# Graph network, first layer: both halves of the features from one window of rows, the own half through DRAM, in a new order of issue

## The chip, the cores and the metric

The kernel runs on one core of one Trainium2 chip. The metric is the device time of one execution in microseconds (us). The time before is the median of seven runs; the profile is one more execution, recorded by the hardware profiler. Engines are named as the profile does: PE (matmul), PEld (its weight load), DVE, ACT, POOL and SP.

## The reference, cut to what matters

There are 12500 nodes with 256 features each and 200000 edges, sorted by destination `dst`. The first layer works in four heads of 32 columns:

```
feat      = relu(x @ W[o] + b[o])          # o = 0: own half (128 columns), o = 1: neighbour half
att_s     = leaky(sum_k feat_self * a_self)          # one number a node and head
att_n     = leaky(sum_k feat_nei  * a_neigh)
edge_w    = (att_s[src] + att_n[dst]) * edge_weight
agg[src] += edge_w * feat_nei[dst]                   # segment sum over edges
y         = concat(headnorm(feat_self), headnorm(agg))
x1        = layernorm(x + y)
```

The second layer computes `relu(x1[src] @ W_a + x1[dst] @ W_b + b)` for each edge, sums it by `dst`, puts the sum and x1 through an update matrix, a relu and two layer norms. So the own half is needed once a node, the neighbour half once an edge, at `dst`.

## The kernel before, in words

Everything runs in three stages one after the other.

**Stage 1, by groups of edges.** The edges are cut into 112 groups (`NG`) of 14 tiles of 128. As edges are sorted by `dst`, all destinations of a group lie in a window of 128 consecutive rows of `x`, which starts at a row number read into a register (`base_reg`, L211). For each group `sort_tasks` (L548) sorts the edges by block of `src`: one-hot tables `A`, `B`, `Z` (`hot` L568, `hot_b` L572, `pair` L576, `reach` L615), counts on PE (`ranks`, `begins`), 14 place look-ups on ACT (`place_pick` L651), the split of a place into quotient and rest (`split` L658 to L660), the one-hot tables of these (`hot_r` L664, `hot_q` L674, `goods` L669), and the target rows `ix` (`index` L644). Then `message` (L718) multiplies a one-hot table `oT` (`hot_n` L709) with the window's neighbour features, `evict` (L725) copies the result out of PSUM, and `scatter` (L731) writes it with four indirect DMAs a group, issued by POOL, to rows `ix` of a log in DRAM. The buffer `ix` has four copies: `index` of group g waits for the scatters of group g-4.

Beside this, `feat_tasks` (L440) computes features. In every step it takes two sets of 128 rows: the window `xw` of group g, for the neighbour half, and block g of 128 nodes `xb`, for the own half. Each is loaded (L432, L438), transposed by PE (L457, L460), copied from PSUM (`keep` L466) and multiplied with its half of the weights (`project` L471, L474). From `relu` (L482) on the two halves lie side by side in one tile of 256 columns: `att_mult` (L486), `mean_sum` (L491), `att_sum` (L495), `centre` (L500). The own half of `F` goes to `selfd` in DRAM by blocks (`out_f` L528), the own attention to the resident tile `atts` (`leaky_s` L525), and the neighbour half is split into three bf16 parts (`part` L514 to L520). There are 112 groups, but only 98 blocks (`NB`): in the last 14 steps there is no `xb`, and the tiles are 128 columns wide.

The order of issue on PE, ACT, DVE and SP is written out by hand: the dictionary `AT` (L40) gives every step of a group a due time, group g stands `TG` = 256 units after group g-1, and all steps are issued in the order of due time:

```
t0 = TG * g
work[t0 + AT[name]].append(f)
for t in sorted(work): ...
```

So one period of 256 units holds one step of each name, of different groups. Every eighth group also brings the steps `m_...`, which prepare the edge lists of the next eight groups. Each engine takes its instructions in that order and waits where an operand is not there yet.

**Stage 2, by blocks of nodes.** For each block of 128 nodes the log is read back (`log_load` L951), expanded (`log_hot` L959, L964) and summed by PE (`log_sum` L972). Four blocks make a batch: `load_y` (L1076) reads `x` and the own half from `selfd`; `own_s` to `own_d` (L1091 to L1124) normalize the own half; `heads_a` (L983) multiplies the sum with `atts` and adds the rest; then follow norms, the projection for the second layer, and the stores of `x1d` and `pd`.

**Stage 3, the second layer,** gathers rows of `pd` by `src` (L1346), and works by groups of edges again (L1370 to L1424).

The functions that the diff touches, and what calls them:

Of the kernel before, what the change touches and what calls it, by code (L numbers as in the profile page):

```python
# [11 lines left out]
def _warn_once_fixed(msg, *args, **kwargs):  # L12
# [28 lines left out]
    "widen": -453, "hot": -365, "hot_b": -265, "pair": -179, "ranks": -86, "quarter": -64, "rows": -29,  # L41
    "begins": 13, "keep_begins": 55, "keep_v": 51, "shift": 161, "reach": 262, "steps": 227, "steps_keep": 243,
    "steps_low": 256, "target": 313, "index": 400, "place_mm0": 52, "place_mm1": 63, "place_mm2": 204,
    "pick0": 73, "pick1": 78, "pick2": 78, "pick3": 87, "pick4": 123, "pick5": 144, "pick6": 156, "pick7": 170,
    "pick8": 179, "pick9": 219, "pick10": 229, "pick11": 239, "pick12": 249, "pick13": 280, "split": 339,
    "hot_r": 358, "goods": 374, "hot_q": 371, "permute": 424, "rel_keep": 435, "extras": 477, "rel_turn": 502,
    "rel_row": 552, "rel_out": 574, "rel_in": 595, "hot_n": 959, "message0": 997, "evict0": 1053,
    "message1": 1032, "evict1": 1063, "message2": 1056, "evict2": 1082, "message3": 1065, "evict3": 1121,
    "message4": 1101, "evict4": 1165, "message5": 1188, "evict5": 1203, "scatter0": 1120, "scatter1": 1146,
    "scatter2": 1197, "scatter3": 1206, "load": -331, "transposes": 47, "keep": 68, "project": 80, "relu": 295,  # L50
    "att_mult": 355, "mean_sum": 459, "att_sum": 438, "centre": 467, "leaky_n": 498, "part0": 584, "part1": 636,
    "part2": 665, "part3": 705, "leaky_s": 585, "out_f": 634, "m_load": -1689, "m_cast0": -1234,
    "m_cast1": -1433, "m_col0": -1201, "m_keep0": -1125, "m_col1": -698, "m_keep1": -614, "m_col2": -941,
    "m_keep2": -861, "m_block": -1073, "m_place": -877, "m_high": -378, "m_rest": -285, "m_mid": 263,
    "m_low": 351, "m_win": -76, "m_turn": -866, "m_pairs": -710, "m_mask": -535, "m_count": 210,
# [45 lines left out]
def kernel(  # L101
# [45 lines left out]
    selfd = dram.tile([ROWS, HD], FT, name="selfd")  # L147
# [12 lines left out]
    atts = consts.tile([P, NB, H], FT, name="atts")  # L160
# [49 lines left out]
    def base_reg(g):  # L210
        return nc.sync.value_load(basei[0:1, g:g + 1], min_val=0, max_val=N - P)  # L211
# [4 lines left out]
    with ExitStack() as l0:  # L216
# [208 lines left out]
        xb = {}  # L425
        F3 = {}

        def load_group(g):
            if g < NG:
                b = base_reg(g) if g else 0  # L430
                xw[g] = xin.tile([P, D], FT, name="xw")
                nc.sync.dma_start(xw[g], x[bass.ds(b, P), :])  # L432
            if g < NB:
                xb[g] = xin.tile([P, D], FT, name="xb")
                n = min(P, N - g * P)
                if n < P:
                    nc.vector.memset(xb[g], 0.0)
                nc.sync.dma_start(xb[g][:n], x[g * P:g * P + n, :])  # L438

        def feat_tasks(g):  # L440

            ww, bb = g < NG, g < NB
            o0, o1 = (0 if bb else 1), (2 if ww else 1)
            lo, hi = o0 * HD, o1 * HD
            st = {}

            def flat(t):
                return t[:, lo:hi]

            def heads(t):  # L450
                return t[:, lo:hi].rearrange("p (a k) -> p a k", k=32)

            def transposes():
                tp = ps.tile([P, 512], FT, name="tp", bufs=1)
                if ww:
                    for c in range(2):
                        nc.tensor.transpose(tp[:, c * P:(c + 1) * P], xw[g][:, c * P:(c + 1) * P], ident)  # L457
                if bb:
                    for c in range(2):
                        nc.tensor.transpose(tp[:, (2 + c) * P:(3 + c) * P], xb[g][:, c * P:(c + 1) * P], ident)  # L460
                st["tp"] = tp

            def keep():
                xT = feat.tile([P, 4, P], FT, name="xT")
                a, z = (0 if ww else 2), (4 if bb else 2)
                nc.scalar.copy(xT[:, a:z].rearrange("p c q -> p (c q)"), st["tp"][:, a * P:z * P])  # L466
                st["xT"] = xT

            def project():
                fp = bank[g][:, 0:D] if ww else ps.tile([P, 512], FT, name="fs")[:, 0:D]  # L470
                nc.tensor.matmul(fp[:, lo:hi], ones3, bias3[:, lo:hi], start=True, stop=False)  # L471
                for o in range(o0, o1):
                    for c in range(2):
                        nc.tensor.matmul(  # L474
                            fp[:, o * HD:(o + 1) * HD], st["xT"][:, (2 + c) if o == 0 else c, :],
                            w0s[:, c, o * 4:(o + 1) * 4, :].rearrange("p a k -> p (a k)"),
                            start=False, stop=(o == o1 - 1 and c == 1))
                st["fp"] = fp

            def relu():  # L480
                st["R"] = feat.tile([P, D], FT, name="R")
                nc.scalar.activation(flat(st["R"]), st["fp"][:, lo:hi], AF.Relu)  # L482

            def att_mult():
                st["tm"] = feat.tile([P, D], FT, name="tm")
                nc.vector.tensor_tensor(flat(st["tm"]), flat(st["R"]),  # L486
                                        atb.rearrange("p o h k -> p (o h k)")[:, lo:hi], op=OP.mult)

            def mean_sum():
                st["m"] = feat.tile([P, 2 * H], FT, name="m")  # L490
                nc.vector.tensor_reduce(st["m"][:, o0 * H:o1 * H], heads(st["R"]), AX.X, OP.add)  # L491

            def att_sum():
                st["a"] = feat.tile([P, 2 * H], FT, name="a")
                nc.vector.tensor_reduce(st["a"][:, o0 * H:o1 * H], heads(st["tm"]), AX.X, OP.add)  # L495

            def centre():
                st["F"] = feat.tile([P, D + H], FT, name="F", bufs=4)
                m = st["m"][:, o0 * H:o1 * H]
                nc.vector.scalar_tensor_tensor(  # L500
                    heads(st["F"]), m[:, :, None].to_broadcast([P, (o1 - o0) * H, 32]), -1.0 / 32, heads(st["R"]),
                    op0=OP.mult, op1=OP.add)

            def leaky_n():
                a = st["a"][:, H:2 * H]
                nc.vector.scalar_tensor_tensor(st["F"][:, D:D + H], a, 0.2, a, op0=OP.mult, op1=OP.max)


            def part(k):
                def f():  # L510
                    n = st["F"][:, HD:]
# [11 lines left out]
            def leaky_s():  # L523
                a = st["a"][:, 0:H]
                nc.vector.scalar_tensor_tensor(atts[:, g, :], a, 0.2, a, op0=OP.mult, op1=OP.max)  # L525

            def out_f():
                nc.sync.dma_start(selfd[g * P:(g + 1) * P, :], st["F"][:, 0:HD])  # L528

            w = lambda f: f if ww else None  # L530
            k = lambda f: f if bb else None
            return dict(transposes=transposes, keep=keep, project=project, relu=relu,
                        att_mult=att_mult, mean_sum=mean_sum, att_sum=att_sum, centre=centre, leaky_n=w(leaky_n),
                        part0=w(part(0)), part1=w(part(1)), part2=w(part(2)), part3=w(part(3)),
                        leaky_s=k(leaky_s), out_f=k(out_f))
# [262 lines left out]
        work = defaultdict(list)  # L798
        for name, fs in (("hot_b", (first_nodes, lambda: load_group(1), load_norm_consts, bias_parts, bases)),
# [4 lines left out]
            work[min(AT[name], AT["split"] - 1) + 0.5] += fs  # L804
# [5 lines left out]
        for g in range(max(NG, NB)):  # L810
            t0 = TG * g
            if g < NG:
                for name, f in sort_tasks(g).items():
                    put_in(t0, name, f)
# [4 lines left out]
            if g % GC == 0 and 0 < g < NG:  # L819
# [98 lines left out]
    with ExitStack() as bar:  # L918
# [64 lines left out]
        def heads_a(q):  # L983
# [4 lines left out]
                                    atts[:, b:b + n, :, None].to_broadcast([P, n, H, 32]), op=OP.mult)  # L988
# [87 lines left out]
        def load_y(q):  # L1076
            b, n = spans[q]
            y = ys[q] = bw.tile([P, BB, D], FT, name="y", bufs=4)
            fs[q] = bw.tile([P, BB, HD], FT, name="fs")
            m = min(n, N // P - b)  # L1080
            if m < n:
                nc.vector.memset(y[:, m], 0.0)
                nc.sync.dma_start(y[:N % P, m], x[(b + m) * P:N, :])
            if m:
                nc.sync.dma_start(y[:, :m], x[b * P:(b + m) * P, :].rearrange("(b p) w -> p b w", p=P))
            nc.sync.dma_start(fs[q][:, :n], selfd[b * P:(b + n) * P, :].rearrange("(b p) w -> p b w", p=P))
# [4 lines left out]
        def own_s(q):  # L1091
            b, n = spans[q]
            own[q] = bw.tile([P, BB, HD], FT, name="oq", bufs=1), bw.tile([P, BB * H], FT, name="ov")
            nc.scalar.activation(own[q][0][:, :n], fs[q][:, :n], AF.Square)
# [12 lines left out]
        def own_c(q):  # L1107
            b, n = spans[q]
            v = own.pop(q)[1]
            F3 = fs[q][:, :n].rearrange("p b (h k) -> p (b h) k", h=H)  # L1110
            nc.vector.reciprocal(v[:, :n * H], v[:, :n * H])
            nc.vector.tensor_tensor(F3, F3, v[:, :n * H, None].to_broadcast([P, n * H, 32]), op=OP.mult)
# [6 lines left out]
        def own_d(q):  # L1119
            b, n = spans[q]  # L1120
            F = fs.pop(q)[:, :n]
# [569 lines left out]
```

## Time and profile before

| what | value |
|---|---|
| median of 7 runs | 4378.88 us (4370.61 to 4387.98) |
| the profiled execution's own time | 4374.71 us |
| its span, first to last instruction | 4372.8 us, so 1.9 us lie around it |
| stage 1, to the first matmul of stage 2 | 0 to 1081 us |
| stage 2, to its last matmul L972 | 1081 to 1992 us |
| stage 3, first L1424 to last instruction | 2019 to 4373 us |
| whole span, busy | PE 84%, DVE 72%, ACT 54%, POOL 61% |
| stage 1 from 50 to 1040 us, busy | PE 96%, DVE 97%, ACT 99%, POOL 53%, granted clock 1.00 |
| stage 2, busy | PE 100%, DVE 95%, ACT 24%, POOL 67%, granted clock 1.00 |
| stage 3, busy | PE 75%, DVE 54%, ACT 47%, POOL 63%, granted clock 0.87 |

In such a table a busy share is the union of the times in which some instruction of the engine runs. Two instructions of one engine overlap by some tens of nanoseconds in the records, so what an instruction costs its engine is the time from its start to the start of the next one; this is read from the timeline, where each line has start, duration, engine, source line, operation, output and inputs.

### The profile page before, as it was taken

The numbers are of one execution on the slowest core, as the hardware profiler recorded it, in microseconds if no ns is written. First come the engines' busy times: TensorE is split into PE (matmuls) and PEld (weight loads), VectorE is DVE, ScalarE is ACT, GpSimd is POOL, SyncE is SP. The second block draws the span as 40 slices with busy tenths as digits, with TensorE's granted clock in tenths as the row PEclk, the third lists the DMA queues.
The fourth block names the chain that finished last, engine by engine and source line by source line (L and its number), as shares of the span: only waits on it lengthen the run. The fifth ranks groups of instructions, "written<-read, shape, count | busy, mean of one in ns | idle before, by whom it ended". The sixth has DMA issues, their size and how long they took to land. (4 is left out here: it accounts for less than half of the span.)

```text
span 4372.8 us, 82564 instructions
## 1 busy us (share of the span) xinstructions
PE 3684.7 (84%) x24976; PEld 3120.0 (71%) x24976; DVE 3165.7 (72%) x9205; ACT 2374.0 (54%) x8379; POOL 2657.8 (61%) x2542
## 2 busy tenths in 40 slices
PE   8999999997999999996777777777777777777776
PEld 6888888876888888885666666666666666666665
DVE  9999999997999999995555555555555555555555
ACT  8999999996122222223444444444444444444444
POOL 2555455555666666664666666666666666666664
PEclk9999999998999999998888888889889888888888
DMA  6777766666666666664555555555555555555554
GB/s 200 273 271 265 250 220 214 216 203 222 180 192 192 191 191 191 189 187 134 143 143 148 145 144 143 147 144 142 146 144 147 145 143 146 144 146 143 144 145 113
DMA packets 470160, 763.55 MB, mean 175 GB/s; under 512 B 76203, under 2 KB 313505, under 8 KB 469713
## 3 DMA queue, kind: packets, MB, share of 16 engines
q1 hardware_dynamic: 339552, 415.13, 33.0%
q0 software_dynamic: 110848, 327.87, 24.4%
q10 hardware_dynamic: 19312, 15.21, 1.1%
q8 instruction: 204, 3.34, 0.3%
q14 instruction: 244, 1.99, 0.1%
HBM read 559.81 MB, written 198.12 MB: 173 GB/s over the span
## 5 line engine op out<-in xcount | busy, mean ns | idle before, releaser
L1346 POOL DMA_INDIRECT gb<-pd,srcf x1563 | 1500.7, 960 | 857.0 <-issue 505.9
L1424 PE MATMUL agg<-gb,o 128*128 128x256 f32 x3126 | 938.8, 428 | 286.0 <-ACT gb L1407 200.6
L1405 DVE TENSOR_TENSOR gb<-qp,gb 128x512 f32<-128x512 f32 x781 | 531.6, 681 | 651.1 <-remote 146.9
L1424 PEld LDWEIGHTS agg<-gb,o 128*128 128x128 f32 x3126 | 645.5, 215 | 458.3 <-ACT gb L1407 253.0
L731 POOL DMA_INDIRECT log<-m,ix x448 | 542.0, 1210 | 528.7 <-ACT m L725 149.9
L972 PE MATMUL sum<-lg,o 128*128 128x256 f32 x3724 | 838.9, 379 | 12.4 <-DVE o L964 12.2
L1407 ACT ACTIVATE gb<-gb 128x512 f32<-128x512 f32 x781 | 487.2, 627 | 631.2 <-DVE gb L1405 412.3
L972 PEld LDWEIGHTS sum<-lg,o 128*128 128x128 f32 x3724 | 696.4, 189 | 112.1 <-POOL lg L959 11.9
L964 DVE TENSOR_SCALAR o<-iotap,lg 128x128 f32<-128x128 f32 x1862 | 612.8, 398 | 42.8 <-PE sum L972 33.6
L651 ACT ACTIVATE junk<-wp,nbig 128x99 bf16<-128x99 f32 x1568 | 602.6, 458 | 0.8 <-PE wp L624 0.7
L1383 PE MATMUL qp<-qh,oT 128*128 128x256 f32 x1563 | 592.9, 398 | 6.2 <-PE agg L1424 1.7
L959 POOL TENSOR_TENSOR lg<-lg 128x512 f32<-128x512 f32 x392 | 431.7, 1114 | 227.8 <-DMA lg<-log 162.6
L651 ACT ACTIVATION_READ_ACCUMULATOR junk<-wp,nbig 128x1 f32 x1568 | 474.1, 315 | 0.0
L1383 PE MATMUL qp<-ql,oT 128*128 128x256 f32 x1563 | 436.6, 299 | 0.6 <-issue 0.6
L718 PE MATMUL mp<-F,oT 128*128 128x132 bf16 x5376 | 416.8, 222 | 19.3 <-DVE oT L709 5.4
L1387 DVE TENSOR_TENSOR o<-iotac,rel 128x256 f32<-128x256 f32 x390 | 161.6, 414 | 321.9 <-PE agg L1424 94.3
L718 PEld LDWEIGHTS <-oT 128*128 128x128 bf16 x5376 | 342.3, 98 | 50.8 <-issue 15.7
L725 ACT COPY m<-mp 128x396 f32<-128x396 f32 (+1 forms) x672 | 350.1, 566 | 10.9 <-PE mp L718 8.2
L1383 PEld LDWEIGHTS qp<-qh,oT 128*128 128x128 f32 x1563 | 329.3, 211 | 35.4 <-PE agg L1424 8.0
L1391 ACT ACTIVATE o<-iotac,rel 128x128 f32<-128x128 f32 x782 | 267.8, 391 | 154.2 <-PE up L1222 52.3
L1383 PEld LDWEIGHTS qp<-ql,oT 128*128 128x128 f32 x1563 | 328.2, 210 | 24.5
L890 PE MATMUL qm<-wms,xT 128*128 128x256 f32 x224 | 97.6, 526 | 272.4 <-ACT xT L885 206.1
(263 smaller groups left out, 6551.1 us busy)
## 6 DMA issues: line engine op xcount, KB each, us to landing
lg<-log SPq DMA_DIRECT2D x392, 268.0 KB
dr<-in_dst_dram SPq DMA_DIRECT2D x781, 128.0 KB
rr<-reld SPq DMA_DIRECT2D x112, 512.0 KB
log<-zero SPq DMA_DIRECT2D x101, 268.0 KB
gb<-pd,srcf POOLq DMA_INDIRECT x1563
lg<-log SPq DMA_DIRECT2D x98, 201.0 KB
xw<-in_x_dram SPq DMA_DIRECT2D x112, 128.0 KB
xw<-x1d SPq DMA_DIRECT2D x112, 128.0 KB
```

Of the source, the lines that this page charges most:

```text
L651: nc.scalar.activation(small("junk", NBX, BF, p=P), st["w", i][:, k * NBE:k * NBE + NBX], AF.Relu, bias=nbig, accum_out=st["sl"][:, t:t + 1])
L718: nc.tensor.matmul(mp[:, r * (HD + H):(r + 1) * (HD + H)], st["oT"][:, r0 + r], F3[g][:, k], start=(k == 0), stop=(k == 2))
L725: nc.scalar.copy(st["m"][:, r0:r0 + n, 0:HD + H], st.pop(("mp", i))[:, :n * (HD + H)].rearrange("p (r w) -> p r w", r=n))
L731: ins = nc.gpsimd.indirect_dma_start(out=log[:, :], out_offset=bass.IndirectOffsetOnAxis(ap=st["ix"][:, k:k + 1], axis=0), in_=st["m"][:, ...
L959: e.tensor_tensor(t[:, 1, :n, 0:HD].rearrange("p r (h k) -> p r h k", h=H), t[:, 0, :n, 0:HD].rearrange("p r (h k) -> p r h k", h=H), t[:, ...
L964: nc.vector.tensor_scalar(o[:, r], iotap, t[:, 0, r, MW - 2:MW - 1], t[:, 0, r, MW - 1:MW], op0=OP.is_equal, op1=OP.mult)
L972: nc.tensor.matmul(sums[b], o[:, r], t[:, :, r, 0:HD], start=(k == 0 and r == 0), stop=(k == NK - 1 and r == n - 1))
L1346: nc.gpsimd.indirect_dma_start(out=gb[s][:r, i], out_offset=None, in_=pd[:, :], in_offset=bass.IndirectOffsetOnAxis(ap=srci[:r, t:t + 1], ...
L1383: nc.tensor.matmul(qp[:r, i], oT[:, i * P:i * P + r], q, start=(k == 0), stop=(k == 1))
L1405: nc.vector.tensor_tensor(z, qp, z, op=OP.add)
L1407: nc.scalar.activation(z, z, AF.Relu)
L1424: nc.tensor.matmul(agg[g], o[:r, i], z[:r, i], start=(j == 0 and i == 0), stop=lastmm)
```

## The change

The block of rows `xb` is gone. Both halves are computed from the window `xw` of the group; windows overlap, so a row of the own half may be computed and written twice with the same values. The loop runs over the 112 groups alone, all of them 256 columns wide. The own half and the own attention lie side by side in `F` and go to `selfd` together, 132 numbers a row, at a row number from the register. Stage 2 reads both back and takes the attention from there; `atts` is gone. `AT` has new numbers throughout.

```diff
 AT = {
-    "widen": -453, "hot": -365, ... "split": 339,
-    "index": 400, ... "mean_sum": 459, "att_sum": 438, "centre": 467, ... "leaky_s": 585, "out_f": 634,
-    "hot_n": 959, "message0": 997, ... "scatter3": 1206, "load": -331, ...
+    "widen": -305, "hot": -253, ... "split": 378,
+    "index": 425, ... "mean_sum": 331, "att_sum": 498, "centre": 535, ... "leaky_s": 641, "out_f": 966,
+    "hot_n": 1017, "message0": 1071, ... "scatter3": 1301, "load": -460, ...
 }
-    selfd = dram.tile([ROWS, HD], FT, name="selfd")
+    selfd = dram.tile([ROWS, H + HD], FT, name="selfd")
-    atts = consts.tile([P, NB, H], FT, name="atts")
         def load_group(g):
-            if g < NG:
-                b = base_reg(g) if g else 0
-                xw[g] = xin.tile([P, D], FT, name="xw")
-                nc.sync.dma_start(xw[g], x[bass.ds(b, P), :])
-            if g < NB:
-                xb[g] = xin.tile([P, D], FT, name="xb")
-                ...
-                nc.sync.dma_start(xb[g][:n], x[g * P:g * P + n, :])
+            xreg[g] = base_reg(g) if g else 0
+            xw[g] = xin.tile([P, D], FT, name="xw")
+            nc.sync.dma_start(xw[g], x[bass.ds(xreg[g], P), :])
             def transposes():
-                if bb:
-                    for c in range(2):
-                        nc.tensor.transpose(tp[:, (2 + c) * P:(3 + c) * P], xb[g][:, c * P:(c + 1) * P], ident)
             def keep():
-                nc.scalar.copy(xT[:, a:z].rearrange("p c q -> p (c q)"), st["tp"][:, a * P:z * P])
+                nc.scalar.copy(st["xT"].rearrange("p c q -> p (c q)"), st["tp"][:, 0:D])
             def project():
-                for o in range(o0, o1):
-                    for c in range(2):
-                        nc.tensor.matmul(
-                            fp[:, o * HD:(o + 1) * HD], st["xT"][:, (2 + c) if o == 0 else c, :],
-                            w0s[:, c, o * 4:(o + 1) * 4, :].rearrange("p a k -> p (a k)"),
-                            start=False, stop=(o == o1 - 1 and c == 1))
+                for c in range(2):
+                    nc.tensor.matmul(fp, st["xT"][:, c, :], w0s[:, c].rearrange("p a k -> p (a k)"),
+                                     start=False, stop=(c == 1))
             def leaky_s():
                 a = st["a"][:, 0:H]
-                nc.vector.scalar_tensor_tensor(atts[:, g, :], a, 0.2, a, op0=OP.mult, op1=OP.max)
+                nc.vector.scalar_tensor_tensor(st["F"][:, 0:H], a, 0.2, a, op0=OP.mult, op1=OP.max)
             def out_f():
-                nc.sync.dma_start(selfd[g * P:(g + 1) * P, :], st["F"][:, 0:HD])
+                nc.sync.dma_start(selfd[bass.ds(xreg[g], P), :], st["F"][:, 0:H + HD])
-        for g in range(max(NG, NB)):
+        for g in range(NG):
         def heads_a(q):
-                                    atts[:, b:b + n, :, None].to_broadcast([P, n, H, 32]), op=OP.mult)
+                                    fs.pop(q)[:, :n, 0:H, None].to_broadcast([P, n, H, 32]), op=OP.mult)
         def load_y(q):
-            fs[q] = bw.tile([P, BB, HD], FT, name="fs")
+            f = fs[q] = bw.tile([P, BB, H + HD], FT, name="fs", bufs=3)
```

The other steps of stage 2 take columns 4 to 131 of `fs` where they took 0 to 127, and the last batch reads its 84 rows with a transfer of its own. In the changed kernel's order of issue, the due times of a period on DVE are: `hot`, `att_mult`, `centre`, `extras`, `hot_b`, `steps_low`, `part1`, `pair`, `mean_sum`, `split` (three instructions), `leaky_s`, `hot_r`, `leaky_n`, `hot_q`, `index`, `goods`, `shift` (two), `reach`, `part3`, `rows`, `att_sum`, `hot_n`. Before, `mean_sum` stood directly ahead of `centre` of the same group, and between `split` and `hot_r` stood `att_mult`.

## The prediction

> **What bounds the kernel now.** I read the windows by stage first: what the change touches lies in stage 1, apart from some operands of stage 2.
>
> ```profile
> 50.00:1040.00 990.00, 950.74 (x11778) 807.48 (x11776) 964.42 (x3030) 980.35 (x4894) 520.99 (x429) 1.00 0.70 238
> 1081.00:1992.00 911.00, 909.24 (x4281) 789.22 (x4282) 869.15 (x2412) 214.81 (x504) 611.70 (x520) 1.00 0.65 188
> 2019.00:4372.00 2353.00, 1758.86 (x8355) 1469.97 (x8353) 1260.37 (x3534) 1117.36 (x2731) 1492.28 (x1555) 0.87 0.52 143
> ```
>
> The columns are length, then busy time of PE, PEld, DVE, ACT and POOL, granted clock, DMA share, GB/s. Stage 2 is PE's: 909 of 911 us, all of it sums that the change leaves alone. Stage 1 is shared: PE 96%, DVE 97%, ACT 99%. Busy shares so close don't say who leads, so I read the waits of DVE from 200 to 900 us.
>
> ```profile
> DVE ix L644 <- DMA log<-m,ix: 2.1, 2, 1.0
> DVE ix L644 <- issue: 1.7, 1, 1.7
> DVE mf L336 <- issue: 0.3, 1, 0.3
> DVE rows L591 <- issue: 0.2, 1, 0.2
> ```
>
> In 700 us DVE waits 4.3 us for others. Its remaining 3% are gaps that it makes itself, as its timeline shows (start, duration):
>
> ```profile
> 503.62 0.41 DVE L495 TENSOR_REDUCE a<-tm 128x8 f32<-128x256 f32 x1
> 503.94 0.74 DVE L709 TENSOR_SCALAR oT<-rr,pcol 128x2048 bf16<-128x2048 bf16 x1
> 504.60 0.29 DVE L520 TENSOR_TENSOR F<-F,F 128x132 bf16<-128x132 f32 x1
> 504.81 0.41 DVE L491 TENSOR_REDUCE m<-R 128x8 f32<-128x256 f32 x1
> 505.25 0.43 DVE L500 SCALAR_TENSOR_TENSOR F<-m,R 128x256 f32<-128x256 f32 x1
> 505.60 0.18 DVE L697 COPY m<-mp 128x16 f32<-128x16 f32 x1
> ...
> 1018.11 0.27 DVE L495 TENSOR_REDUCE a<-tm 128x4 f32<-128x128 f32 x1
> 1018.30 0.74 DVE L709 TENSOR_SCALAR oT<-rr,pcol 128x2048 bf16<-128x2048 bf16 x1
> ...
> 1019.20 0.28 DVE L491 TENSOR_REDUCE m<-R 128x4 f32<-128x128 f32 x1
> 1019.52 0.29 DVE L500 SCALAR_TENSOR_TENSOR F<-m,R 128x128 f32<-128x128 f32 x1
> ```
>
> L495 holds DVE 0.32 us (503.62 to 503.94), the equal L491 0.44 us: what follows it reads its result. So DVE is the engine that stage 1 goes by. `goods` L669 starts at 102.34 us for group 8 and at 927.30 for group 97: 9.27 us a group. The medians of start-to-start of one group's instructions add up to 8.49 us, the `m_` steps to 5.4 us in eight groups, 0.67 each; less 0.03, because they stand behind L491 in a quarter of the groups. DVE's own work is thus 9.13 us, its waits 0.14. In the last groups, with 128 columns, L495 takes 0.19 us, and groups 97 to 109 follow each other in 8.83 us.
>
> **The change, part by part.**
>
> *PE and ACT lose work.*
>
> ```profile
> L474 PE MATMUL fs<-w0s,xT 128*128 128x128 f32 x660 | 96.8, 288 | 0.5
> L466 ACT COPY xT<-tp 128x512 f32<-128x512 f32 x78 | 50.2, 643 | 4.8 <-PE fs L640 4.7
> L460 PE MATMUL tp<-ident,xb 128*128 128x128 f32 x156 | 29.8, 273 | 0.0
> ```
>
> These are 200 to 1000 us, by form. Two transposes go: 29.8 / 78 = 0.38 us a group. Eight passes of L474 at 96.8 / 660 = 0.147 us become four of 256 columns, at the 838.9 / 3724 = 0.225 us of L972: 1.17 to 0.90. PE saves 0.65 us a group. `keep` holds ACT 0.48 us (start to start); at 256 columns I take 0.28, as L466 has in the last groups: 0.20 saved. Both lie beside DVE's 9.13 us and are worth nothing by themselves. That cover is thick: DVE would have to lose over 0.3 us a group before ACT led again, since ACT fills 8.7 to 8.8 us in the last groups, where it is 98 to 100% busy, and gets 0.1 back from the wider relu.
>
> *DVE keeps every instruction in 98 groups.* The order changes two neighbourhoods. `mean_sum` no longer stands ahead of its `centre`: 0.44 - 0.33 = 0.11 us, in 80 of 105 groups, so -0.08. Between `split` and `hot_r`, which reads its result, now stands the tiny `leaky_s`. A dependent pair of that size (L659, L660) takes 0.21 us; L660 and `leaky_s` independently 0.09 + 0.08; so +0.04. Own work: 9.09. The waits depend on the new order and can't be read from the old trace: between 0 and twice 0.14. I take 0.14, because every wait of the old kernel has a counterpart in the new order, while PE and ACT have more room: 9.23 us. Over 97 groups: -0.04 x 97 = -4 us (bounds -17 and +10).
>
> *The last 14 groups get wider on DVE:* four operations of 256 columns and one `leaky_s`. They go from 8.83 to 9.23 us: 14 x 0.40 = +5.6 us.
>
> The Trainium skill's page "VectorE: DVE Perf Modes", section "The DRAIN you can't avoid", says that a semaphore after each of eight copies costs nothing, the total being the same as without. The pair above, 0.44 against 0.32 us, says that a dependent neighbour does cost. By the page the new order would gain nothing there, and the sum would be 4 us higher; I go by the rows.
>
> *Transfers.* SP issues one load a group less (128 KB), and stores 132 instead of 128 numbers a row, 14 times more often. The DMA share in stage 1 is 0.70 and SP issues about six transfers in 9.27 us at some 0.4 us each, so none of this is on the path: 0. The store's place matters: `out_f` (966) now stands on SP directly ahead of `rel_in` (970 = 714 + 256), and behind `rel_in` wait `hot_n` and all messages. It waits for `leaky_s` (641), 325 units earlier, and for the store one group before it, because addresses from a register may overlap: both long done. One period is 256 units of 36 ns, so `rel_in` has 303 units, 11 us, to `hot_n`; in the drain, where nothing else hides it, issue to use took 4.2 us (1057.87 to 1062.07). `load` to `transposes` grows from 378 to 557 units. Cost 0.
>
> The page "DMA: Bandwidth & Descriptors", section "How a descriptor splits into AXI transactions", speaks against rows of 528 bytes: starting off the 256-byte grid, each needs one or two transactions more than a row of 512. No row of this trace shows it; as an estimate by that page a 66 KB store would weigh like 100 KB, still less than the load that goes, so the sum stays.
>
> *Start and drain.* Up to the first `goods` (30.06 us) DVE has the same work plus one `mean_sum`, 0.33 us; `rows` of group 0 now waits for PE and ACT about 1 us, where before DVE stood 0.72 + 0.28 us at two later places. In the drain POOL's scatters run back to back in both. I take 0, within 2 us.
>
> *Stage 2* reads the attention from `fs` in strides of 132; PE hides it (909 of 911 us): 0. Reads of `selfd` now wait for all its stores, but the first log rows anyway wait for the last scatters: 0.
>
> Sum: 4374.7 - 4 + 5.6 = 4376.3 us for the profiled execution. It lies 4.2 us under the median of the seven, so 4380 us: 0.03% from before, where a measurement of this kernel can tell about 0.2%, 8.8 us.
>
> **The rivals.**
>
> *Faster: the waits go.* PE and ACT run ahead of DVE once they have 0.65 and 0.2 us to spare, and no operand is late. Then a group takes 9.09 us: -0.18 x 97 = -17, the last 14 groups +0.26 x 14 = +4: 4366 us. For it: much of the 0.14 us is DVE held up for moments by ACT, such as L698 before `rows`, 0.17 instead of 0.12 us in a tenth of the groups. Against it: the longest waits, some 4 us in all, are `index` behind a DMA, which the change doesn't help. Chance 0.20.
>
> *Slower: `index` waits for the scatters.* Its buffer comes free when the scatters of group g-4 have landed. By due times the distance from the fourth scatter shrinks from 400 + 1024 - 1206 = 218 to 425 + 1024 - 1301 = 148 units, by 2.5 us.
>
> ```profile
> L731 POOL DMA_INDIRECT log<-m,ix x448 | 542.0, 1210 | 528.7 <-ACT m L725 149.9 <-ACT rT L693 137.9 <-ACT rs L686 78.2
> ```
>
> Before, 3.7 to 7.0 us, 5.6 on average, lay between the end of the fourth scatter and `ix`. In nine groups 3.7 to 3.8 us did without a wait, so rows usually land by then; in five it took 4.9 to 6.3. If ACT keeps its lag to the plan, 5.6 - 2.5 = 3.1 us are left, and each group lacks 0.6 us. A wait also moves the next `ix` away, so half remains: 0.3 x 108 = +32 us, 4412. If ACT runs ahead to where `hot_n` holds it, the path from `hot_n` through `message`, ACT's 5.2 us to the fourth `evict` and two scatters takes some 10 of the 15.8 us to `ix`; over 5 us are left and nothing waits. It decides below 3.7 us. I think the second end nearer, as ACT gets slack; a case in between is 4400 us. Chance 0.30.
>
> *Slower: PE's clock.* PE's share falls to (8.9 - 0.65) / 9.23 = 89%. Granted clock is 1.00 at 92% (900 to 1000 us), but 0.87 in stage 3 at 75%. At 0.87 PE would need 8.25 / 0.87 = 9.5 us, +0.27 x 112 = +30: 4410. Chance 0.04.
>
> **How the numbers follow.** No change to tell (4370 to 4388) has 0.46; faster 0.20; slower 0.34, from the two slower rivals. The range leaves a tenth at each end: 4366, the end of the faster rival, to 4410, nearly the full price of the waits. The likeliest case alone lies in 4370 to 4390.
>
> **What would show it.** Right: `goods` every 9.2 us from the first group to the last; DVE 98% busy in stage 1, PE near 89%, ACT 96%; `centre` and `mean_sum` apart, 0.33 us each. Wrong: `ix` waiting for the DMA in most groups (slower rival); a period under 9.12 (faster); a clock under 0.95 before 1040 us; or `hot_n` waiting for `rr`, which would say that the new SP order matters.

## The result, and the profile after

The changed kernel takes 4388.95 us (median of 14 runs) against 4377.41 us (34 runs) for the kernel before: 11.5 us more, a ratio of 1.0026 with a 95% interval of 1.0019 to 1.0033. That is inside the range of the prediction, but not the case it held likeliest: the change costs a little more than the 0.2% that the prediction took as the least that can be told from nothing.

The profiled execution after has a span of 4388.2 us, 15.4 us more than before. The first sum of stage 2 starts at 1096.4 us instead of 1080.9, and the rest of the span is 3291.8 us instead of 3291.9. So all of it is in stage 1. (The medians differ by 11.5 us; the profiled execution before took 4374.7 us, 2.7 under its median, the one after 4390.0 us, 1.0 over it.) The windows by stage (length, busy time of PE, PEld, DVE, ACT and POOL, granted clock, DMA share, GB/s):

```profile
50.00:1040.00 990.00, 933.37 (x11015) 767.39 (x11014) 965.31 (x2995) 958.93 (x4811) 510.14 (x422) 0.99 0.67 224
1097.00:2007.00 910.00, 908.35 (x4282) 787.76 (x4280) 872.02 (x2412) 215.23 (x505) 611.47 (x520) 1.00 0.64 188
2034.00:4388.00 2354.00, 1760.62 (x8354) 1470.70 (x8352) 1254.75 (x3533) 1119.61 (x2730) 1493.65 (x1554) 0.88 0.52 143
```

In stage 1 two of the three busy engines lose share in the same 990 us: PE has 94% (before 96%), ACT 97% (before 99%). DVE keeps its 97.5% although the groups get longer; an instruction that takes longer counts as busy for longer, so the share can't show such a loss. `goods` (now L642) says where the time is. These are the lines of groups 8, 97 and 109:

```profile
101.65 1.31 DVE L642 TENSOR_TENSOR mv<-rh,em 128x1120 bf16<-128x1120 bf16 x1
...
934.62 1.31 DVE L642 TENSOR_TENSOR mv<-rh,em 128x1120 bf16<-128x1120 bf16 x1
...
1047.19 1.31 DVE L642 TENSOR_TENSOR mv<-rh,em 128x1120 bf16<-128x1120 bf16 x1
```

A group takes 9.36 us up to group 97 (before 9.27) and 9.38 us after it (before 8.83): 0.09 x 89 = 8 us and 0.55 x 12 = 6.6 us. From group 109 to the first sum of stage 2 it is 1.5 us more, up to group 8 it is 0.7 us less.

DVE's time from group 8 to 97 is split much as in the prediction: the median start-to-start time of each pair of neighbouring instructions is its own work, what exceeds the medians is waiting. Own work goes from 9.15 to 9.12 us a group, waiting from 0.12 to 0.24 (the prediction had 9.13 and 0.14 for the kernel before). The neighbourhood term is in DVE's timeline (start, duration): `mean_sum`, L466, now releases DVE after 0.33 us, where it took 0.44 us ahead of its `centre`.

```profile
690.67 0.42 DVE L466 TENSOR_REDUCE m<-R 128x8 f32<-128x256 f32 x1
691.00 0.18 DVE L631 SCALAR_TENSOR_TENSOR sl<-sl,twin 128x14 f32<-128x14 f32 x1
```

The waits of DVE, 200 to 900 us (total, times, longest), are 5.0 us instead of 4.3:

```profile
DVE ix L617 <- DMA log<-m,ix: 1.4, 3, 0.6
DVE rows L564 <- ACT junk L624: 1.4, 3, 0.8
DVE ix L617 <- PE mp L691: 1.1, 6, 0.2
DVE sl L631 <- ACT junk L624: 0.7, 2, 0.4
DVE rows L564 <- issue: 0.4, 1, 0.4
```

They explain little of 0.12 us a group. The excess over the medians, added up by pair of neighbours over 89 groups, shows more: 6.0 us ahead of `ix`, 5.3 us between `q` (L632) and `r` (L633) of `split`, 3.4 us ahead of `rows`, 1.6 us between `sl` and `q`. In the kernel before, the pair `q`, `r` had almost none, 0.3 us, while the pair ahead of `ix` had 4.4 us already. So the largest new term is that of `q` and `r`. A time lost between two instructions of one engine, with no wait listed, is an instruction that itself takes longer:

```profile
643.74 0.18 DVE L632 TENSOR_SCALAR q<-sl 128x14 bf16<-128x14 f32 x1
...
691.21 0.36 DVE L632 TENSOR_SCALAR q<-sl 128x14 bf16<-128x14 f32 x1
```

The same 14 numbers a partition take 0.18 or 0.36 us. That became one of the questions for the experiments.

### The profile page after: what moved, and what is told of

Same layout as the page of the kernel before. It is cut to its first block, busy times and chain, and to the rows that moved or that the text cites. A ratio compares the mean times of both kernels' runs of the same rounds, so it can differ in the third digit from the quotient of the medians.

```text
span 4388.2 us, 81541 instructions
## 1 busy us (share of the span) xinstructions
PE 3688.9 (84%) x24388; PEld 3095.3 (71%) x24388; DVE 3179.1 (72%) x9219; ACT 2370.3 (54%) x8379; POOL 2658.6 (61%) x2542
## 5 line engine op out<-in xcount | busy, mean ns | idle before, releaser
L624 ACT ACTIVATE junk<-wp,nbig 128x99 bf16<-128x99 f32 x1568 | 557.4, 375 | 3.2 <-PE wp L597 2.5
L624 ACT ACTIVATION_READ_ACCUMULATOR junk<-wp,nbig 128x1 f32 x1568 | 361.2, 231 | 0.0
L698 ACT COPY m<-mp 128x396 f32<-128x396 f32 (+1 forms) x672 | 295.7, 476 | 16.5 <-PE mp L691 11.9
```

Source lines behind the costliest of these rows:

```text
L624: nc.scalar.activation(small("junk", NBX, BF, p=P), st["w", i][:, k * NBE:k * NBE + NBX], AF.Relu, bias=nbig, accum_out=st["sl"][:, t:t + 1])
L698: nc.scalar.copy(st["m"][:, r0:r0 + n, 0:HD + H], st.pop(("mp", i))[:, :n * (HD + H)].rearrange("p (r w) -> p r w", r=n))
```

## The experiments

The kernels ran in three sets of four, each set on one chip together with the kernel before; every ratio is to the kernel before on the same chip. This matters: the kernel before itself took 4375.3, 4403.9 and 4009.2 us (medians) on the three chips.

### Is it the order or the rows?

The change does two things. Three kernels take them apart.

**The rows alone**: the changed kernel with the old table of due times.

```diff
-    "widen": -305, "hot": -253, "hot_b": -214, "pair": -196, "ranks": -50, "quarter": -24, "rows": -22,
+    "widen": -453, "hot": -365, "hot_b": -265, "pair": -179, "ranks": -86, "quarter": -64, "rows": -29,
...
```

> The changed kernel with the due times of the kernel before: one set of rows a group and the longer rows stay, the order of issue is undone. Two theories of the 11.5 us. Order: the new order meets more short waits of DVE (0.24 us a group where the old one had 0.12), worth 8 us over the groups with an own half. Then this kernel goes back to 9.27 us a group there, keeps the wider last 14 groups (+5 to +7 us), and takes some +6 us over the kernel before: 4383 us, ratio 1.0014. Rows: the store of 132 numbers in every group or the load by register brings the waits, whatever the order. Then it stays at +11 us or gains DVE's 0.04 us a group from mean_sum standing ahead of centre again: 4389 to 4393 us, ratio 1.0026 to 1.0035.

Measured: 4374.82 us, ratio 1.0001 (0.9992 to 1.0009). The rows theory is out, and the order theory's 4383 us was too high as well. DVE runs with 0.04 us of waiting a group, 9.17 us from group to group. Its waits from 200 to 900 us are two:

```profile
DVE ix L616 <- DMA log<-m,ix: 0.4, 1, 0.4
DVE ix L616 <- PE mp L690: 0.4, 1, 0.4
```

**The order alone**: the kernel before with the new table.

```diff
-    "widen": -453, "hot": -365, "hot_b": -265, "pair": -179, "ranks": -86, "quarter": -64, "rows": -29,
+    "widen": -305, "hot": -253, "hot_b": -214, "pair": -196, "ranks": -50, "quarter": -24, "rows": -22,
...
```

> The kernel before with the due times of the changed kernel: two sets of rows a group as before, only the order is new. Order theory: 9.36 us a group with an own half instead of 9.27, last 14 groups narrow as before: +8 us, 4385 us, ratio 1.0018; with PE and ACT still loaded with the second set of rows it may be more, up to +15 us. Rows theory: the order alone costs no wait and gains 0.04 us a group on DVE: 4373 us, ratio 0.9990.

Measured: 4393.88 us against 4375.32 on that chip, ratio 1.0047 (1.0033 to 1.0061): 18.6 us, a little past the 15 us of the order theory's dear end. DVE's own work is 9.12 us, the waiting 0.27 us a group.

**The wider last groups alone**, in the kernel before:

```diff
-            o0, o1 = (0 if bb else 1), (2 if ww else 1)
+            o0, o1 = 0, (2 if ww else 1)
...
-                            fp[:, o * HD:(o + 1) * HD], st["xT"][:, (2 + c) if o == 0 else c, :],
+                            fp[:, o * HD:(o + 1) * HD], st["xT"][:, (2 + c) if o == 0 and bb else c, :],
```

> The kernel before, with the features of the last 14 groups computed over all 256 columns (the own half of these groups is computed and not used). It prices the wider last groups alone. By start to start of DVE's instructions, the four operations cost 0.39 us a group more there; the group goes from 8.83 to some 9.25 us: +5.5 us, 4383 us, ratio 1.0013. Rival: in these groups ACT, 98 to 100% busy, sets the pace, and DVE's wider operations fill its gaps: under +2 us, ratio 1.0003.

Measured: 4378.73 us, ratio 1.0010 (1.0001 to 1.0019): 4 us, between the two expectations. Groups 97 to 109 take 9.20 us instead of 8.83, which over 14 groups is 5.2 us.

The table that these make (ratio to the kernel before):

| | old order | new order |
|---|---|---|
| two sets of rows a group | 1 | 1.0047 |
| one set of rows a group | 1.0001 | 1.0026 |

The new order costs 0.25% with one set of rows and 0.47% with two. The single set of rows has wider last groups, which cost 0.10% by themselves, but no loss shows with it in the old order, and in the new order it saves some 0.2%. So what the change loses it loses to the order.

### Why does q take 0.36 us?

From group 8 to 97 of the changed kernel, 37 `q`, two in five, took over 0.28 us; before none did. In all 37 a scatter was running on POOL that ended 0.02 us after `q` did. One such group, first in DVE's timeline, then in POOL's:

```profile
681.46 0.52 DVE L549 TENSOR_TENSOR B<-A 128x693 bf16<-128x693 bf16 x1
681.89 0.41 DVE L466 TENSOR_REDUCE m<-R 128x8 f32<-128x256 f32 x1
682.22 0.17 DVE L631 SCALAR_TENSOR_TENSOR sl<-sl,twin 128x14 f32<-128x14 f32 x1
682.42 0.36 DVE L632 TENSOR_SCALAR q<-sl 128x14 bf16<-128x14 f32 x1
682.81 0.17 DVE L633 TENSOR_TENSOR r<-sl,q 128x14 bf16<-128x14 f32 x1
```

```profile
681.35 1.45 POOL L704 DMA_INDIRECT log<-m,ix  x1 [0.30 <-ACT junk L624]
```

The scatter ends at 682.80 and `q` at 682.78. The test computes `q` by a form with two tensors (`magic` holds MAGIC * NR in all 14 columns):

```diff
-                nc.vector.tensor_scalar(q, sl, MAGIC * NR, -MAGIC * NR, op0=OP.add, op1=OP.add)
+                nc.vector.scalar_tensor_tensor(q, sl, MAGIC * NR, magic, op0=OP.add, op1=OP.subtract)
```

> The changed kernel with q of split computed by another form of instruction: (sl + M) - M with the second M read from a tensor, SCALAR_TENSOR_TENSOR in place of TENSOR_SCALAR, the same result. In the changed kernel this instruction took 0.36 us instead of 0.18 in some 40% of the groups, each time one that began 0.6 to 1.2 us after the start of a scatter on POOL, and the scatter ended with it. Port theory: the one-tensor form holds a port of SBUF that POOL's descriptor writing needs too, and each holds up the other; the two-tensor form does not. Then its longest durations go to 0.20 us, the 6.8 us that they add over 89 groups go, and the whole kernel gains 5 to 8 us: 4381 us, ratio to the kernel before 1.0012. Rival: whatever stands there on DVE is held up, or the scatter then holds the next instruction: the loss moves to r or hot_r and the time stays at 4388 us, ratio 1.0028.

Measured: ratio 1.0014 (1.0005 to 1.0023), against 1.0026 (1.0019 to 1.0033) for the changed kernel: 5 us gained, if two ratios with overlapping intervals are compared. The trace is plainer than the time. No `q` takes over 0.22 us, and the mean of its group from 200 to 900 us is 177 ns instead of 253:

```profile
L632 DVE TENSOR_SCALAR q<-sl 128x14 bf16<-128x14 f32 x75 | 18.9, 253 | 2.9
```

```profile
L634 DVE SCALAR_TENSOR_TENSOR q<-sl,magic 128x14 bf16<-128x14 f32 x76 | 13.4, 177 | 3.0
```

Here is the same situation again, with the scatter starting 0.87 us before `sl`:

```profile
899.09 0.17 DVE L633 SCALAR_TENSOR_TENSOR sl<-sl,twin 128x14 f32<-128x14 f32 x1
899.29 0.17 DVE L634 SCALAR_TENSOR_TENSOR q<-sl,magic 128x14 bf16<-128x14 f32 x1
```

```profile
898.22 1.45 POOL L706 DMA_INDIRECT log<-m,ix  x1 [0.30 <-ACT junk L626]
```

The scatter takes 1.45 us in both, so `q` had not been holding it up: `q` was held until POOL was nearly done. The second kernel had 25 `q` with 0.34 to 0.43 us of a scatter left when they began, and none was held. Neither does the loss move to `r` (174 ns in both). The rival is out.

The Trainium skill's page "SBUF — State Buffer", section "SBUF: two separate sides", says that DVE and POOL share one pair of ports, that it is an exclusive lock between an instruction of POOL and one of DVE that needs the pair, and that whichever starts first holds it for the whole instruction. A lock would fit these rows; that it lasts for all of the scatter that the trace records does not. At 643.74 us `q` took 0.18 us in the midst of a scatter that ran from 643.43 to 644.39:

```profile
643.43 0.96 POOL L704 DMA_INDIRECT log<-m,ix  x1 [2.84 <-ACT m L698]
```

The slow ones all began when 0.34 to 0.43 us of the scatter, as the trace records it, were left, and those with under 0.25 or over 0.5 us left were hardly held up.

So the loss is a question of phase: which instruction of DVE falls on that stretch of a scatter. In the old order, with one set of rows or with two, `q` fell outside it in every group.

The phase is no accident. A scatter that begins while `pair` (L549) runs on DVE, or shortly before, takes longer than the usual 0.96 us, 0.99 to 1.60, and ends 0.83 us after `pair` does: 41 of 41 in the changed kernel that began from 0.25 us before `pair` to 0.14 us before its end. In 28 of the 37 slow cases the scatter was one of these, and `q` began 0.45 us after the end of `pair`, with 0.38 us left, as in the rows above: 681.98, 682.42, 682.80. In the old order `split` stands directly behind `pair`. One group of the changed kernel in that order, DVE and POOL:

```profile
503.63 0.52 DVE L548 TENSOR_TENSOR B<-A 128x693 bf16<-128x693 bf16 x1
504.06 0.21 DVE L630 SCALAR_TENSOR_TENSOR sl<-sl,twin 128x14 f32<-128x14 f32 x1
504.31 0.17 DVE L631 TENSOR_SCALAR q<-sl 128x14 bf16<-128x14 f32 x1
```

```profile
503.60 1.42 POOL L703 DMA_INDIRECT log<-m,ix  x1 [2.06 <-ACT rT L665]
```

Here `q` begins 0.16 us after `pair` ends, with 0.71 us of the scatter left, and is not held. The new order puts `mean_sum`, 0.33 us, between the two. So the move that saves 0.11 us ahead of `centre` also brings `q` to the end of the scatter. This is read from the traces; no run moves `mean_sum` alone.

### Is the rest the wait of ix?

**Eight buffers for `ix`**, so that it can't wait for scatters.

```diff
-                nc.vector.tensor_tensor(small("ix", RW, I32, bufs=4, p=P), st["sm"][:, 4:4 + RW], roww, op=OP.add)
+                nc.vector.tensor_tensor(small("ix", RW, I32, bufs=8, p=P), st["sm"][:, 4:4 + RW], roww, op=OP.add)
```

> The changed kernel with eight buffers for ix instead of four, so that index cannot wait for scatters. If that wait is part of the loss, DVE's excess ahead of L617, 5.2 us over 88 groups, goes: -3 to -6 us against the changed kernel, 4384 us, ratio to the kernel before 1.0015. If it only stands in for a wait that comes next (or if the gap is the sums on PE that index reads), nothing changes: 4388 us, ratio 1.0025.

Measured: 4388.77 us, ratio 1.0033 (1.0020 to 1.0046), no gain. The excess ahead of `ix` falls from 6.0 to 2.7 us over 89 groups, and the group from 9.36 to 9.33 us; the last groups lost it again (9.55 us). Room for `ix` alone brings nothing that shows.

**Longer leads** for what DVE waits for, with `q` mended.

```diff
-    "widen": -305, "hot": -253, "hot_b": -214, "pair": -196, "ranks": -50, "quarter": -24, "rows": -22,
+    "widen": -305, "hot": -253, "hot_b": -214, "pair": -196, "ranks": -64, "quarter": -46, "rows": -10,
...
-    "steps_low": 301, "target": 388, "index": 425, "place_mm0": 82, "place_mm1": 120, "place_mm2": 266,
+    "steps_low": 301, "target": 340, "index": 425, "place_mm0": 82, "place_mm1": 120, "place_mm2": 266,
...
-    "pick7": 255, "pick8": 274, "pick9": 289, "pick10": 289, "pick11": 294, "pick12": 345, "pick13": 358,
-    "split": 378, "hot_r": 391, "goods": 439, "hot_q": 420, "permute": 523, "rel_keep": 538, "extras": 553,
+    "pick7": 255, "pick8": 274, "pick9": 289, "pick10": 289, "pick11": 294, "pick12": 330, "pick13": 340,
+    "split": 384, "hot_r": 393, "goods": 439, "hot_q": 420, "permute": 523, "rel_keep": 538, "extras": 553,
```

> The changed kernel in its new order, with q from two tensors, and with a few due times moved by 6 to 48 units (36 ns each) so that the three instructions of DVE that wait for others stand further behind what they read: quarter 22 units earlier with ranks 14 earlier, rows 12 later; target 48 earlier ahead of index; pick12 and pick13 15 and 18 earlier, split 6 later. Lead theory: what is left of the loss in the new order after q is mended (ratio 1.0014) is that these leads are shorter than in the old order (quarter to rows 2 units against 35, pick13 to split 20 against 59, target to index 37 against 87): the 11 us of excess ahead of ix, sl and rows go for the most part and the ratio falls to 0.999 to 1.0005. Rival: the leads don't matter, the engines drift into other waits of the same size: 1.0014 as without them.

Measured: ratio 1.0083 (1.0069 to 1.0096), far worse than both expectations. Longer leads of this kind don't pay; as they brought new waits with them, the run doesn't settle what the short leads cost. DVE's waits from 200 to 900 us:

```profile
DVE ix L619 <- DMA log<-m,ix: 9.1, 8, 3.1
DVE tm L462 <- ACT R L458: 8.1, 18, 0.8
DVE ix L619 <- PE tp L342: 0.4, 1, 0.4
```

The waits ahead of `rows` and `sl` are gone, as meant. But `att_mult`, due 4 units after `relu`, now waits for it. One reason may lie in the table: `ranks`, at 192 of a period's 256 units instead of 206, has moved ahead of `project`, at 203, on PE, and `relu` reads `project`. And `ix` does wait for scatters, up to 3.1 us. What one wait lost others more than took.

What is left of the order's cost after `q`, some 6 us, I can therefore not pin to one wait. The waits of ACT and PE give only a hint of the side on which it lies. With one set of rows, first in the old order, then in the new:

```profile
ACT R L457 <- DVE dw L607: 5.0, 12, 0.6
ACT R L457 <- DVE A L544: 2.3, 4, 0.6
```

```profile
ACT rows L560 <- PE fs L557: 5.4, 8, 0.9
ACT rs L659 <- PE fs L602: 5.3, 14, 0.8
```

In the old order ACT waits for DVE, as it should where DVE leads. In the new order it waits mostly for sums of PE, and what ACT loses there can come back to DVE at `rows` and `sl`. PE's own row from 200 to 900 us in the new order, which the old order lacks, names a step that was moved:

```profile
PE fs L602 <- ACT R L458: 8.8, 25, 0.7
```

L602 is `steps`. It writes the same PSUM tile that `relu` reads (`bank[g]`), and is due at 287, 22 units behind `relu` at 265; in the old table it stood at 227, ahead of `relu` at 295. In 71 of 89 groups it began within 0.1 us of the end of `relu`, in the old order in none. The kernel with longer leads left both due times as they were, and no run moves them apart. So it stays open whether this is the step, and whether DVE's loss comes from it.

### Versions that go faster

If DVE's own work sets the pace in the old order, less of it must show in the time. All of these are the changed kernel in the old order.

**One leaky instruction**: with one set of rows both halves' attention lies in one tile, so a single instruction can write both.

```diff
-                a = st["a"][:, H:2 * H]
-                nc.vector.scalar_tensor_tensor(st["F"][:, H + D:], a, 0.2, a, op0=OP.mult, op1=OP.max)
+                a = st["a"].rearrange("p (o h) -> p o h", o=2)
+                nc.vector.scalar_tensor_tensor(st["FF"][:, :, 0:H], a, 0.2, a, op0=OP.mult, op1=OP.max)
```

> The changed kernel in the old order, with leaky_n and leaky_s as one instruction over both halves, at the place of leaky_n. DVE theory: in the old order DVE goes by its own work (9.13 of 9.17 us a group), so that a small instruction less, 0.07 us start to start, is worth 0.07 x 112 = 8 us: 4367 us, ratio to the kernel before 0.998. Rival: ACT or the waits take it up, as the old order has only 0.04 us of waits and they are not proof of slack: 4375 us, ratio 1.000.

Measured: ratio 0.998 (0.9971 to 0.9989), as DVE's theory had it. Own work falls to 9.05 us a group; the one profile has 0.13 us of waiting, where the old order without this edit had 0.04. With `q` from two tensors as well:

```diff
-                nc.vector.tensor_scalar(q, sl, MAGIC * NR, -MAGIC * NR, op0=OP.add, op1=OP.add)
+                nc.vector.scalar_tensor_tensor(q, sl, MAGIC * NR, magic, op0=OP.add, op1=OP.subtract)
```

> The changed kernel in the old order with one leaky instruction for both halves and q from two tensors. Beside the kernel with one leaky alone, at 0.998: q is rarely held up in the old order (0.6 us in 89 groups), so the port theory expects 0.998 again, at most 1 us better; if the two-tensor form were better for another reason, 0.0005 to 0.001 lower.

Measured: ratio 0.9989 (0.9980 to 0.9998). The intervals of the two overlap: no gain shows from the other form of `q` where no `q` falls on the end of a scatter.

**The subtractions on POOL**:

```diff
-                        nc.vector.tensor_tensor(n, n, F3[g][:, 0], op=OP.subtract)
+                        nc.gpsimd.tensor_tensor(n, n, F3[g][:, 0], op=OP.subtract)
...
-                        nc.vector.tensor_tensor(F3[g][:, 2], n, F3[g][:, 1], op=OP.subtract)
+                        nc.gpsimd.tensor_tensor(F3[g][:, 2], n, F3[g][:, 1], op=OP.subtract)
```

> The changed kernel in the old order, with part1 and part3 (two subtractions of 128 x 132 numbers a group) on POOL instead of DVE. POOL is 53% busy in stage 1. DVE theory without the port: DVE loses 2 x 0.20 us start to start a group, so that ACT leads at some 8.9 us: -0.27 x 112 = -30 us, 4345 us, ratio 0.993. Port theory: POOL's subtractions and DVE's one-tensor instructions hold each other up, and scatters wait on POOL behind them; the gain is eaten in part or in whole: 4365 to 4400 us, ratio 0.998 to 1.006, with hot_n, hot and Z on DVE longer than before.

Measured: ratio 0.9996 (0.9987 to 1.0004): nothing. DVE's own work falls only to 8.96 us a group, where 2 x 0.20 us less would be 8.73, and the waiting rises to 0.31. The groups of POOL, then of DVE, 200 to 900 us (busy time, mean ns of one, idle time before):

```profile
L494 POOL TENSOR_TENSOR F<-F,F 128x132 f32<-128x132 f32 x75 | 51.3, 684 | 7.0 <-ACT F L492 4.7 <-ACT xT L446 0.5 <-issue 0.2
```

```profile
L681 DVE TENSOR_SCALAR oT<-rr,pcol 128x2048 bf16<-128x2048 bf16 x75 | 61.1, 814 | 0.0
L540 DVE TENSOR_TENSOR A<-iotab,bx 128x693 bf16<-128x693 bf16 x75 | 46.1, 615 | 0.0
```

With the subtractions on DVE, the same two:

```profile
L681 DVE TENSOR_SCALAR oT<-rr,pcol 128x2048 bf16<-128x2048 bf16 x76 | 56.8, 747 | 0.0
L540 DVE TENSOR_TENSOR A<-iotab,bx 128x693 bf16<-128x693 bf16 x76 | 38.9, 512 | 0.0
```

`hot`, L540, takes 615 ns on average, against 512 with the subtractions on DVE. In 47 of 75 groups a subtraction on POOL ran beside it, and there it took 0.68 us; in the other 28 it took 0.51. `hot_n` goes from 747 to 814. Here instructions of DVE with two tensors are held up too.

**Half of `pair`**:

```diff
-                st["B"] = srt.tile([P, h, NBX], BF, name="B")
-                nc.vector.tensor_tensor(st["B"], st["A"][:, :h], st["A"][:, h:], op=OP.add)
-                st["C"] = [st["B"][:, i] for i in range(h)]
+                w, A = 4, st["A"]
+                st["B"] = srt.tile([P, w, NBX], BF, name="B")
+                nc.vector.tensor_tensor(st["B"], A[:, :w], A[:, h:h + w], op=OP.add)
+                st["C"] = [st["B"][:, i] for i in range(w)] + [A[:, i + o] for o in (0, h) for i in range(w, h)]
```

`h` is 7; `ranks` and `begins` run over the ten entries of `C`.

> The changed kernel in the old order, with pair adding four of the seven pairs of rows only; the other six rows go to ranks and begins as they are, three passes more in each. DVE's B shrinks from 693 to 396 elements a partition, about 0.18 us less a group; PE gets six short passes more, 6 x 0.07 = 0.4 us. DVE theory: PE needs some 8.3 us of 9.17 and takes them; -0.18 x 112 = -20 us, 4355 us, ratio 0.9954, or less if ACT leads first at 8.9 to 9.0 us a group. Rival: PE's passes lie on the way from pair to begins and index, and rows or ix waits: 4375 us or more, ratio 1.000 to 1.003.

Measured: ratio 0.9987 (0.9978 to 0.9995), a third of what was expected. DVE's own work did fall by 0.15 us, to 8.98, but the waiting rose to 0.21: with `pair` shorter, `split` starts earlier, and 22 of 90 `q` now fall on the end of a scatter (3.8 us in 89 groups). All three together:

> The changed kernel in the old order with one leaky instruction for both halves (0.998 alone), pair over four of seven pairs (0.9987 alone) and q from two tensors. If the gains add, as DVE still goes by its own work: 0.07 + 0.15 us less own work a group, and the 3.8 us that q lost to the port in the half-pair kernel: ratio 0.996, 17 us under the kernel before. Rival: ACT leads by then, or waits for PE's six passes more: 0.9975 to 0.999.

Measured: 3996.23 us against 4009.23 on that chip, ratio 0.9966 (0.9952 to 0.9980). This is what the two gains give together (0.998 x 0.9987 = 0.9967), without a further one from `q`. It is the fastest version here, 13 us under the kernel before. Own work is 8.93 us a group, from group to group 9.06.

**The kernel before, once more**, on the chip of the last four:

> The kernel before, unchanged, on the same chip as the other three: a ratio of 1.000 within 0.001, and a profile that shows how far DVE's excess (0.12 us a group in the first profile) and the end of stage 1 (1080.9 us) vary from one execution to another: I expect 0.08 to 0.16 us and 1077 to 1084 us.

Measured: ratio 1.0002 (0.9993 to 1.0011). But its profile has 0.07 us of waiting a group and ends stage 1 at 1074.1 us, under what I expected. Two profiles of one kernel, on two chips, differ by 7 us at the end of stage 1. So a few us between two profiles say nothing by themselves, and neither do a few hundredths of a microsecond of waiting a group.

## Why the prediction was right or wrong

**DVE leads stage 1**: right. Its own work is 9.12 of 9.36 us a group, and in the old order 0.07 us less of it was worth 0.1 to 0.2% of the time in two measurements. Where its own work fell further, waits took most of that back: 0.15 us less with half of `pair` gave 0.13%, 0.17 us less with POOL's help nothing.

**The neighbourhoods, -0.04 us**: right, -0.03. The 0.44 us ahead of `centre` became 0.33. The Trainium skill's page "VectorE: DVE Perf Modes", section "The DRAIN you can't avoid", has a semaphore cost nothing in eight copies; here a neighbour that reads the result cost 0.11 us more than one that doesn't.

**The waits, "I take 0.14, because every wait of the old kernel has a counterpart in the new order"**: this is the step that failed. They are 0.24 us, near the upper bound of 0.28 that the text gave. A counterpart is not the same wait: in the new order `q` fell on the end of a scatter in two groups of five, 5 us in all, a cost that I had not listed. PE came to stand behind `relu` and ACT behind PE; what that costs DVE was not shown. This term turned the planned -4 us into +8. The range held because the waits had been given a bound of +10 us, not because their cause was known.

**The last 14 groups, 8.83 to 9.23 us**: the mechanism was right. In the kernel before, in the old order, the widening alone gives 9.20; in the new order the groups take 9.38, so its cost shows there as well.

**PE and ACT "worth nothing by themselves"**: half wrong. PE saved less than planned: four passes of 256 columns take 96.1 / 340 = 0.283 us each, not 0.225, so they cost 1.13 us, hardly under the 1.17 of eight passes. PE is at 94%, not 89%: its busy time fell from 8.94 to 8.84 us a group instead of by 0.65. The passes account for 0.23 of the 0.55 that are missing; the rest is open. One set of rows may still be worth something in the old order beyond its wider last groups (1.0001 against 1.0010, intervals that overlap), by waits that went away (0.04 us a group against 0.07 and 0.12 in two profiles of the kernel before). That would be the faster rival's mechanism; it is not shown.

**The rival of `index`**: did not decide. `ix` waited 1.4 us for the DMA in 700 us, less than before, and eight buffers brought nothing. It needed less than I thought to wake it, though: in the kernel with longer leads it took 9.1 us.

**The clock rival**: wrong, the clock is 0.99 in stage 1. **Transfers, start, drain and stage 2 at nothing**: right. The whole difference is there when stage 2 begins, and none of it at the first `goods` (30.0 us after, 30.06 before); from group 109 to stage 2 it is 49.2 us after and 47.7 before, and the last two groups account for 1.1 us of that. The DMA share of stage 1 fell from 0.70 to 0.67. In the estimate for rows of 528 bytes, a row that starts at a multiple of 16 bytes takes three transactions against two, so one more than a row of 512, not "one or two"; its 100 KB go with one.

**The chances**: 0.46 stood on no change, 0.34 on slower. The ratio missed "no change" by 0.06%, the time by 1 us. So "slower" came true, but by neither of the two rivals that carried its 0.34.

## What to carry to other kernels

A hand-made order is tuned to a phase: which small instruction of DVE falls on the end of a scatter of POOL, which lead an engine has. A change that replaces the whole table loses that, even if every instruction and every dependence is as before; so price the waits of a new order well above those of the old one, and test order and work apart. Where an engine's row of groups shows no wait but its neighbours drift apart, look for instructions whose duration has two values, and for what runs on the other engine at that moment.

## What the runs showed of the hardware

- A TENSOR_SCALAR on DVE of 14 numbers a partition took 0.36 us instead of 0.18 when it began with 0.34 to 0.43 us of an indirect DMA's recorded time left on POOL, 37 times of 37; SCALAR_TENSOR_TENSOR at the same place took 0.17 to 0.18 us, 25 times of 25.
- An indirect DMA on POOL that began while a TENSOR_TENSOR of 693 bf16 numbers a partition ran on DVE took 0.99 to 1.60 us instead of 0.96, and ended 0.83 us after that instruction did, 41 times of 41.
- A subtraction on POOL beside `hot` on DVE, a TENSOR_TENSOR in bf16, made it 0.68 us instead of 0.51.
- The same kernel took 4375, 4404 and 4009 us on three chips. On the third the granted clock in stage 3 was 0.99, on the first 0.87; so compare on one chip only.
